# Row factors of two graph attentions: spread over the partitions by TensorE, or put to DRAM once and read back for every partition

## The chip, the cores and the metric

The kernel runs on one core of a Trainium2 chip. The metric is the device time of one launch in microseconds (us), the median of the runs shown. A profile is of one further execution of the same program; its durations are those of that execution.

## The reference

Two layers act on x, 3327 nodes of 256 features, with one graph of 3327 x 3327. Each layer is a graph attention followed by a feed-forward part. Layer 0's attention has two heads of 128 features, layer 1's one head of 256. What matters here is the attention:

```python
# layer 0 (per head); layer 1 is the same with one head, then elu
e = leaky_relu(s1[:, None, :] + s2[None, :, :], 0.2)     # node i, neighbour j
e = where(adj == 1, e, -9e15)
att = softmax(e, axis=1)
h_prime = einsum("ijh,jhc->ihc", att, W3h)
x = x + h_prime
```

Layer 0 goes on with a mixture of 16 experts, two for each token (`silu(h w1) * (h w2)`, then `w3`). Layer 1 goes on with 30 steps of `h + 0.01 tanh(h)`, `h * sigmoid(h)`, layer norm and a 256 x 256 product.

## The kernel before, in words

The 3327 nodes are padded to 26 tiles of 128 (`NT = 26`). `exp(leaky_relu(s1 + s2))` is split so that no exponential is needed for a pair of nodes: for node i and neighbour j the weight is a product of a factor of i, which softmax cancels, with `relu(full_j * row_i - part_j) + part_j`. `row_i = exp(0.8 s1_i)` is the **row factor**. `Scores.finish` computes `row`, `full`, `part` and `minus` with the node on the partition, 128 x 26 x heads.

`attend` does one attention. Its work is cut into **parts**: a group of tiles of nodes i, for one head. Layer 0 has the groups 0-3, 4-9, 10-15, 16-21, 22-25 with two heads each: ten parts, numbered 0 to 9, of 4, 4, 6, 6, 6, 6, 6, 6, 4, 4 tiles. Layer 1 has nine parts, eight of three tiles and one of two. Within a part a loop of 26 **steps** runs over the tiles j of neighbours. A step is one instruction on ScalarE (`e`, L252), one on VectorE (`pT`, L257, which multiplies by the graph's mask `adjT`) and for each tile of the part a product on TensorE (L262), which is two records in the trace:

```python
e  = relu(rb * full_j + minus_j)        # ScalarE, L252; rb: row factors along the free dimension
pT = (e + part_j) * adjT                # VectorE, L257
po[c] += pT[:, c].T @ wh[j]             # TensorE, L262
```

`e` and `pT` have three buffers each, so ScalarE can be three steps ahead of VectorE and VectorE three ahead of TensorE.

In `e` the node i lies along the free dimension, and every one of the 128 partitions needs the same row factors. `row_factors` makes that tile, `rb`: for each tile a product on TensorE of the factor's column, taken 128 times as the stationary operand, with the identity (L221), into a PSUM bank, and for up to four tiles a copy by ScalarE (L225). `rb` has two buffers. The `rb` of part k+1 is made in step 13 of part k. `rb` buffers also take the gathered tokens of the experts (`gathered`, L730): the first of them is asked for while layer 0's attention is still at work.

The results of a part are closed within the steps of the next (`close`, from step 2 on). When both heads of a group are closed in layer 0, `route` follows: a normalization of the group's tiles into the tile `row` (not the row factors; one buffer), whose variance goes to GpSimd for a power (`rstd`, L120) and comes back to VectorE (L127), then a store of `row` to `table_x`, the gate's products on TensorE (L147, L499), a dozen small operations on VectorE that pick two experts, and for each tile two indirect DMAs from GpSimd that write the tokens into the experts' lists (L565). These are held back and let out one by one between the steps.

The graph comes in by groups. `take_graph` lets GpSimd's queue convert a group's rows from int32 to one byte into a DRAM buffer, `in_bytes` (L301), and SyncE's queue reads them back transposed into `adjT` (L311). The buffer is one, so a group's conversion waits for the transposes of the group before. Groups 0 to 2 are asked for before the attention begins; group 3 and 4 after the last list entries of groups 0 and 1.

In layer 1, SyncE's queue stores each finished group of x to `kept`, before x is normalized in place.

A scheduler turns this into one order for each engine. It works from the program's order and its own estimates; an engine then works strictly in that order, waits included. `keep_in_program_order` binds an instruction to its place among the others of its queue.

Of the kernel before, what the change touches and what calls it, by code (L numbers as in the profile page):

```python
# [11 lines left out]
F32 = mybir.dt.float32  # L12
# [8 lines left out]
P = 128  # L21
# [9 lines left out]
def gat_moe_gat_recurrent_ffn(ctx: ExitStack, tc: tile.TileContext, a: dict, out: bass.AP):  # L31
    nc = tc.nc
    N, D = a["x"].shape
    KD = D // P
    NT = (N + P - 1) // P
# [9 lines left out]
    groups0 = [range(0, 4), range(4, 10), range(10, 16), range(16, 22), range(22, 26)]  # L45
    groups1 = [range(max(t - 2, 0), t + 2) for t in range(0, NT, G)]
    groups2 = [range(t, min(t + 3, NT)) for t in range(0, NT, 3)]
# [3 lines left out]
    def rows(t):  # L51
        return P if t < NT - 2 else (REST + 1 - t % 2) // 2
# [44 lines left out]
    ident = const.tile([P, P], F32, name="ident")  # L97
# [85 lines left out]
    class Scores:  # L183
# [9 lines left out]
        def finish(self, t0, t1):  # L193
            nc.scalar.activation(self.full[:, t0:t1], self.s[:, t0:t1, 1], AF.Exp)
            nc.scalar.activation(self.part[:, t0:t1], self.s[:, t0:t1, 1], AF.Exp, scale=ALPHA)
            nc.scalar.activation(self.row[:, t0:t1], self.s[:, t0:t1, 0], AF.Exp, scale=1.0 - ALPHA)
            nc.vector.tensor_scalar(self.minus[:, t0:t1], self.part[:, t0:t1], -1.0, None, op0=ALU.mult)

    quick = []

    def attend(sc, wh, heads, row_groups, per_bank, finish, finished, pools, later, leave=False):

        work, rows_p, ps_r, ps_o = pools
        W = wh.shape[3]  # L210
        most = max(len(ts) for ts in row_groups)
        parts = [(ts, h) for ts in row_groups for h in range(heads)]

        def row_factors(ts, h):

            rb = rows_p.tile([P, most * P], F32, name="rb")
            for c0 in range(0, len(ts), 4):
                some = ts[c0 : c0 + 4]
                p = ps_r.tile([P, 4, P], F32, name="bank")
                for c, t in enumerate(some):  # L220
                    nc.tensor.matmul(  # L221
                        p[:, c, :], lhsT=sc.row[:, t, h : h + 1].to_broadcast([P, P]), rhs=ident,
                        start=True, stop=True,
                    )
                nc.scalar.copy(  # L225
                    rb[:, c0 * P : (c0 + len(some)) * P], p[:, : len(some), :].rearrange("p c q -> p (c q)")
                )
            return rb

        def close(ts, h, po):  # L230

            for c, t in enumerate(ts):
                pr = rows(t)
                r = small.tile([P, 1], F32, name="r")
                nc.vector.reciprocal(r[:pr], po[c][:pr, W - 1 : W])
                finish(t, pr, h, po[c][:pr, : W - 1], r[:pr])
                yield
            if h == heads - 1:
                yield from finished(ts)

        closing = iter(())
        following = row_factors(*parts[0])
        for k, (ts, h) in enumerate(parts):
            n = len(ts)
            rb = following
            acc = [ps_o.tile([P, 512], F32, name=f"acc{q}") for q in range((n + per_bank - 1) // per_bank)]
            po = [acc[c // per_bank][:, (c % per_bank) * W : (c % per_bank + 1) * W] for c in range(n)]
            for j in range(NT):
                if j == NT // 2 and k + 1 < len(parts):
                    following = row_factors(*parts[k + 1])  # L250
                e = work.tile([P, most * P], F32, name="e")
                nc.scalar.activation(  # L252
                    e[:, : n * P], rb[:, : n * P], AF.Relu,
                    scale=sc.full[:, j, h : h + 1], bias=sc.minus[:, j, h : h + 1],
                )
                pT = work.tile([P, most * P], F32, name="pT")
                masked = nc.vector.scalar_tensor_tensor(  # L257
                    pT[:, : n * P], e[:, : n * P], sc.part[:, j, h : h + 1],
                    adjT[:, j // 2, ts[0] * P : (ts[-1] + 1) * P, j % 2], op0=ALU.add, op1=ALU.mult,
                )  # L260
                for c in range(n):
                    nc.tensor.matmul(  # L262
                        po[c], lhsT=pT[:, c * P : (c + 1) * P], rhs=wh[:, j, h, :],
                        start=(j == 0 and c % per_bank == 0), stop=(j == NT - 1),
                        skip_group_check=True,
                    )
                if j >= 2 and (next(closing, later) is later and later and later[0] in quick or later and j % 2 == 0):
                    later.popleft()(masked.ins)
            for _ in closing:
                pass  # L270
            while later and later[0] in quick:
                later.popleft()(None)
            closing = close(ts, h, po)
        if leave:
            return closing
        for _ in closing:
            pass
        while later:
            later.popleft()(None)
# [42 lines left out]
    dram = ctx.enter_context(tc.tile_pool(name="dram", bufs=1, space=bass.MemoryType.DRAM))  # L322
# [35 lines left out]
    with ExitStack() as moe:  # L358
# [16 lines left out]
        H = 2  # L375
        C = D // H
        keep = moe.enter_context(tc.tile_pool(name="keep0", bufs=1))
        wh = keep.tile([P, NT, H, C + 1], F32, name="wh")
        sc = Scores(keep, H)
        ps = moe.enter_context(tc.tile_pool(name="ps0", bufs=4, space=PSUM))  # L380
        ps_o = moe.enter_context(tc.tile_pool(name="ps0o", bufs=2, space=PSUM))
# [99 lines left out]
        run = moe.enter_context(tc.tile_pool(name="edge0", bufs=3))  # L481
        rows_p = moe.enter_context(tc.tile_pool(name="rows0", bufs=2))
# [131 lines left out]
        row = gate.tile([P, MOST, D], F32, name="row")  # L614
# [111 lines left out]
        def gathered(s):  # L726
            if s % 3 == 0 or s == ALWAYS:
                places.append(rows_p.tile([P, MOST * P], F32, name="rb"))
            row = places[-1][:, (s % 3) * D : (s % 3 + 1) * D]
            nc.gpsimd.indirect_dma_start(  # L730
                out=row, out_offset=None, in_=table_x[: EARLY * P, :] if s < FIRST else table_x,
                in_offset=bass.IndirectOffsetOnAxis(ap=which[:, s : s + 1], axis=0),
            )
            return row
# [113 lines left out]
            weights(0)  # L848

        later = deque()  # L850
        closing = attend(sc, wh, H, groups0, 3, add_scaled, route, (run, rows_p, ps, ps_o), later, True)
        ahead.append(gathered(3))
        weights(1)

# [37 lines left out]
    with ExitStack() as st:  # L892
# [3 lines left out]
        wh = s_wh[:, :, :, 2:]  # L896
        sc = Scores(keep, 1, s_wh[:, :, 0, 0:2].rearrange("p t (s h) -> p t s h", h=1))
        nc.vector.memset(wh[:, :, :, D : D + 1], 1.0)
        work = st.enter_context(tc.tile_pool(name="work2", bufs=2))
        ps = st.enter_context(tc.tile_pool(name="ps2", bufs=2, space=PSUM))  # L900
        ps_o = st.enter_context(tc.tile_pool(name="ps2o", bufs=2, space=PSUM))
# [33 lines left out]
        run = st.enter_context(tc.tile_pool(name="edge2", bufs=3))  # L935
        rows_p = st.enter_context(tc.tile_pool(name="rows2", bufs=2))
        fin = st.enter_context(tc.tile_pool(name="fin2", bufs=2))
# [11 lines left out]
        def begin_state(ts):  # L949
# [3 lines left out]
            tiles = [x[:, t, :] for t in ts]  # L953
            normalized(tiles, tiles, S)

        attend(sc, wh, 1, groups2, 1, add_elu, begin_state, (run, rows_p, ps, ps_o), deque())

# [16 lines left out]
    with ExitStack() as st:  # L976
        ps_t = st.enter_context(tc.tile_pool(name="ps3t", bufs=2, space=PSUM))
        ps_o = st.enter_context(tc.tile_pool(name="ps3o", bufs=2, space=PSUM))
# [13 lines left out]
        for step in range(N_STEPS):  # L992
            for ts in groups:
# [28 lines left out]
                if step == N_STEPS - 1:  # L1022
                    here = slice(ts[0] * P, (ts[-1] + 1) * P)
# [55 lines left out]
```

The softmax here doesn't subtract the row's maximum and nothing guards it: scores larger than these inputs give would overflow.

## Time and profile before

| | |
|---|---|
| Median of 3 runs | 2000.29 us (1998.33 to 2000.75) |
| Profiled execution, its own time | 2004.62 us |
| Its span on the core | 2002.9 us |
| Mean granted clock of TensorE | 0.994 |
| Layer 0's attention, on TensorE | about 50 to 395 us |
| Experts | about 395 to 748 us |
| Layer 1's attention | about 793 to 1096 us |
| 30 steps of the last part | from about 1098 us to the end |

The profile counts busy time by engine, cuts the span into 40 slices of about 50 us, and follows the chain of work that ended last back from the end. In a line of a timeline stand the start, the duration, the engine, the line of the kernel (L221), the operation, the names of what is written and read, the count, and in brackets the idle time ahead of it with what ended it. Queue q0 is GpSimd's DMA queue, q1 SyncE's, q10 ScalarE's.

### The profile page before, as it was taken

How to read it: one execution, taken by the hardware profiler on the slowest of the kernel's cores; microseconds unless marked ns; L12 is line 12 of the kernel's file. 1: busy time of each engine (PE TensorE's matmuls, PEld its weight loads, DVE VectorE, ACT ScalarE, POOL GpSimd, SP SyncE). 2: the span in 40 equal slices, each digit the busy share in tenths (PEclk: the TensorE clock that was granted, in tenths of full speed). 3: DMA queues.
4: the chain of work that ended last, by engine and by line, in shares of the span. 5: the costliest groups of instructions: out<-in, count | busy, mean ns of one | idle time of the engine just before them, and what ended most of it. 6: DMA issues, size and time to landing. Idle time of an engine off the chain costs nothing.

```text
span 2002.9 us, 33524 instructions
## 1 busy us (share of the span) xinstructions
PE 1930.9 (96%) x12032; PEld 1750.0 (87%) x12032; DVE 1299.7 (65%) x3827; ACT 1095.5 (55%) x1419; POOL 938.4 (47%) x864
## 2 busy tenths in 40 slices
PE   7999999999999997999999999999999999999998
PEld 6999999989999986888888888888888888888887
DVE  6887888722222226567576777777777777777777
ACT  2967766621111115566555666666666666666664
POOL 3020212443333321001000787787787787787785
PEclk9999999999999998999999999999999999999999
DMA  8978141189999854000001000000000000000003
GB/s 165 119 100 119 10 76 50 39 291 324 351 330 308 297 195 137 9 8 17 9 17 35 1 1 1 1 1 1 1 1 1 1 1 1 1 1 1 1 1 116
DMA packets 139754, 157.08 MB, mean 78 GB/s; under 512 B 52027, under 2 KB 99364, under 8 KB 139586
## 3 DMA queue, kind: packets, MB, share of 16 engines
q1 hardware_dynamic: 123466, 122.05, 19.8%
q0 software_dynamic: 11440, 28.09, 8.1%
q10 hardware_dynamic: 4680, 4.76, 0.7%
q8 instruction: 98, 1.61, 0.3%
q14 instruction: 70, 0.57, 0.1%
HBM read 164.58 MB, written 29.78 MB: 97 GB/s over the span
## 4 chain that ended last, share of the span: by engine, by line
PE 68%; issue 9%; ACT 5%; POOL 5%; DVE 4%; DMA 3%; SPq 0%; another core or an unknown queue 0%; POOLq 0%; DVEq 0%; ACTq 0%
PE po L1014 35%; PE acc L262 23%; PE pt L1008 5%; ACT zT L1010 5%; DVE pT L257 2%; POOL given L831 2%; POOL rb L730 2%; DMA given<-wh,to 2%; PE bank L786 2%; PE acc L827 1%; PE bank L499 1%; PE bank L221 0%; DVE x L913 0%; PE acc L162 0%; POOL rstd L120 0%
## 5 line engine op out<-in xcount | busy, mean ns | idle before, releaser
L1014 PE MATMUL po<-wc,zT 128*128 128x256 f32 x3120 | 705.5, 383 | 21.7 <-ACT zT L1010 21.1
L1014 PEld LDWEIGHTS po<-wc,zT 128*128 128x128 f32 x3120 | 583.1, 190 | 124.1 <-ACT zT L1010 49.7
L252 ACT ACTIVATE e<-rb,minus,full 128x384 f32<-128x384 f32 (+3 forms) x494 | 400.2, 824 | 180.9 <-DVE pT L257 162.7
L1000 POOL TENSOR_TENSOR th<-th,x 128x1024 f32<-128x1024 f32 (+1 forms) x210 | 460.8, 2213 | 64.3 <-ACT th L998 62.7
L257 DVE SCALAR_TENSOR_TENSOR pT<-e,part,adjT 128x384 f32<-128x384 f32 (+3 forms) x494 | 381.1, 776 | 138.1 <-PE acc L262 117.5
L1019 DVE SCALAR_TENSOR_TENSOR x<-po,rr,bb 128x256 f32<-128x256 f32 x780 | 324.9, 478 | 118.3 <-PE po L1014 113.8
L1010 ACT COPY zT<-pt 128x1024 f32<-128x1024 f32 (+1 forms) x210 | 199.0, 947 | 334.0 <-PE pt L1008 334.0
L1006 DVE BATCH_NORM_STATS2 stats<-z 128x6 f32<-128x256 f32 x780 | 283.7, 415 | 117.6 <-ACT z L1001 117.6
L262 PE MATMUL acc<-wh,pT 128*128 128x129 f32 x2704 | 310.4, 276 | 1.8 <-DVE pT L257 1.8
L262 PEld LDWEIGHTS acc<-wh,pT 128*128 128x128 f32 x2704 | 305.2, 192 | 2.5 <-DVE pT L257 2.4
L262 PE MATMUL acc<-s_wh,pT 128*128 128x257 f32 x1352 | 295.3, 380 | 0.8 <-DVE pT L257 0.7
L262 PEld LDWEIGHTS acc<-s_wh,pT 128*128 128x128 f32 x1352 | 255.9, 190 | 37.7 <-DVE pT L257 1.8
L120 POOL TENSOR_TENSOR rstd<-ve,neg_half 128x4 f32<-128x4 f32 (+3 forms) x28 | 30.4, 1086 | 415.7 <-DVE ve L118 332.1
L989 POOL TENSOR_TENSOR rr<-rr,neg_half 128x4 f32<-128x4 f32 (+1 forms) x210 | 208.0, 990 | 17.4
L1001 ACT ACTIVATE z<-th 128x1024 f32<-128x1024 f32 (+1 forms) x210 | 210.6, 1003 | 0.6 <-POOL th L1000 0.5
L998 ACT ACTIVATE th<-x 128x1024 f32<-128x1024 f32 (+1 forms) x210 | 199.3, 995 | 1.9 <-DVE x L127 0.9
L1008 PE MATMUL pt<-ident,z 128*128 128x128 f32 x1560 | 191.6, 274 | 2.5 <-DVE high L944 2.5
L1008 PEld LDWEIGHTS pt<-ident,z 128*128 128x128 f32 x1560 | 179.5, 142 | 14.9 <-issue 2.9
L786 PEld LDWEIGHTS bank<-hT,wh 128*128 128x128 f32 x1280 | 150.7, 194 | 9.2 <-issue 4.8
L786 PE MATMUL bank<-hT,wh 128*128 128x128 f32 x1280 | 151.8, 277 | 6.6 <-issue 2.2
L820 DVE TENSOR_TENSOR pT<-e,bank 128x512 f32<-128x512 f32 x61 | 41.9, 687 | 176.9 <-PE bank L786 124.2
L816 ACT ACTIVATE e<-bank 128x512 f32<-128x512 f32 x61 | 36.4, 597 | 194.1 <-PE bank L786 90.3
(189 smaller groups left out, 1346.4 us busy)
## 6 DMA issues: line engine op xcount, KB each, us to landing
wh<-in_w_dram SPq DMA_DIRECT2D x120, 512.0 KB
first_set<-in_w_dram SPq DMA_DIRECT2D x63, 512.0 KB
in_bytes<-in_adj_dram POOLq DMA_DIRECT2D x3, 2496.0 KB
x<-in_x_dram SPq DMA_DIRECT2D x6, 512.0 KB
kept<-x SPq DMA_DIRECT2D x8, 384.0 KB
old<-kept SPq DMA_DIRECT2D x6, 512.0 KB
out_dram<-x SPq DMA_DIRECT2D x6, 512.0 KB
table_x<-row ACTq DMA_DIRECT2D x3, 768.0 KB
```

Source lines behind the costliest of these rows:

```text
L252: nc.scalar.activation(e[:, : n * P], rb[:, : n * P], AF.Relu, scale=sc.full[:, j, h : h + 1], bias=sc.minus[:, j, h : h + 1],)
L257: masked = nc.vector.scalar_tensor_tensor(pT[:, : n * P], e[:, : n * P], sc.part[:, j, h : h + 1], adjT[:, j // 2, ts[0] * P : (ts[-1] + 1 ...
L262: nc.tensor.matmul(po[c], lhsT=pT[:, c * P : (c + 1) * P], rhs=wh[:, j, h, :], start=(j == 0 and c % per_bank == 0), stop=(j == NT - 1), s ...
L786: nc.tensor.matmul(p[:, f, :], lhsT=w[:, k, f * P : (f + 1) * P], rhs=hT[:, k, :], start=(k == 0), stop=(k == KD - 1),)
L989: nc.gpsimd.tensor_tensor(r[:, :n], r[:, :n], neg_half[:, :n], ALU.pow)
L1000: nc.gpsimd.tensor_tensor(th[:, :n, :], th[:, :n, :], hs, ALU.add)
L1001: nc.scalar.activation(z[:, :n, :], th[:, :n, :], AF.Silu, scale=1.0 / S)
L1006: nc.vector.bn_stats(stats[:, j, :], z[:, j, :])
L1008: nc.tensor.transpose(pt[:, j, k, :], z[:, j, k * P : (k + 1) * P], ident)
L1010: nc.scalar.copy(zT[:, :n, :, :], pt[:, :n, :, :])
L1014: nc.tensor.matmul(po[:, j, :], lhsT=zT[:, j, k, :], rhs=wc[:, k, :], start=(k == 0), stop=(k == KD - 1),)
L1019: nc.vector.scalar_tensor_tensor(x[:, ts[0] + j, :], po[:, j, :], rr[:, j : j + 1], bb, op0=ALU.mult, op1=ALU.add)
```

## The change

`attend` gets a triple, `spread`: the queue for the row factors, the number of parts that still make `rb` as before (`by_dma`), and a place in SBUF for one small tile (`room`). In layer 0 these are GpSimd's queue, 3 and a slice of the router's tile `row`; in layer 1 SyncE's queue, 1 and a tile `low`.

All row factors of a layer are transposed once by TensorE (52 or 26 rows of 128), copied by VectorE to that place and put to DRAM (`factors`). From part `by_dma` on, `rb` is read from there by one DMA, whose source repeats the same rows for all 128 partitions: 128 x 6 x 128 floats for a part of six tiles, 393 KB. The put stands in step 2 of part `by_dma - 1`; the read of the first such part in step 13 of the part before, later ones in step 2 of the part before.

```diff
-    def attend(sc, wh, heads, row_groups, per_bank, finish, finished, pools, later, leave=False):
+    def attend(sc, wh, heads, row_groups, per_bank, finish, finished, pools, later, spread, leave=False):
...
+        queue, by_dma, room = spread
+        factors = dram.tile([NT * heads, P], F32, name=f"factors{heads}")
+
+        def put_factors():
+
+            p = ps_r.tile([P, 512], F32, name="bank")[: NT * heads, :P]
+            nc.tensor.transpose(p, sc.row.rearrange("p t h -> p (t h)"), ident)
+            lines = room()[: NT * heads, :P]
+            nc.vector.tensor_copy(lines, p)
+            tc.keep_in_program_order(queue.dma_start(factors, lines))
 
         def row_factors(ts, h):
 
             rb = rows_p.tile([P, most * P], F32, name="rb")
+            if parts.index((ts, h)) >= by_dma:
+                here = factors[ts[0] * heads + h : ts[0] * heads + h + 1, :]
+                queue.dma_start(
+                    rb[:, : len(ts) * P].rearrange("p (c q) -> p c q", q=P),
+                    bass.AP(tensor=here.tensor, offset=here.offset, ap=[[0, P], [heads * P, len(ts)], [1, P]]),
+                )
+                return rb
...
             for j in range(NT):
-                if j == NT // 2 and k + 1 < len(parts):
+                if j == 2 and k == by_dma - 1:
+                    put_factors()
+                if j == (NT // 2 if k < by_dma else 2) and k + 1 < len(parts):
                     following = row_factors(*parts[k + 1])
...
-        closing = attend(sc, wh, H, groups0, 3, add_scaled, route, (run, rows_p, ps, ps_o), later, True)
+        closing = attend(sc, wh, H, groups0, 3, add_scaled, route, (run, rows_p, ps, ps_o), later, (nc.gpsimd, 3, lambda: row[:, 0, :]), True)
...
-        attend(sc, wh, 1, groups2, 1, add_elu, begin_state, (run, rows_p, ps, ps_o), deque())
+        attend(
+            sc, wh, 1, groups2, 1, add_elu, begin_state, (run, rows_p, ps, ps_o), deque(),
+            (nc.sync, 1, lambda: fin.tile([P, D], F32, name="low")),
+        )
```

## The prediction

> **What bounds the kernel now.** I read the page's busy shares first, then the 40 slices, then the chain that ended last, then stretches of the timeline of TensorE (PE), VectorE (DVE) and GpSimd (POOL) around the row factors.
>
> ```profile
> PE 1930.9 (96%) x12032; PEld 1750.0 (87%) x12032; DVE 1299.7 (65%) x3827; ACT 1095.5 (55%) x1419; POOL 938.4 (47%) x864
> DMA  8978141189999854000001000000000000000003
> ...
> PE po L1014 35%; PE acc L262 23%; PE pt L1008 5%; ACT zT L1010 5%; DVE pT L257 2%; POOL given L831 2%; POOL rb L730 2%; DMA given<-wh,to 2%; PE bank L786 2%; PE acc L827 1%; PE bank L499 1%; PE bank L221 0%; DVE x L913 0%; PE acc L162 0%; POOL rstd L120 0%
> ...
> L221 PE MATMUL bank<-ident,row 128*128 128x128 f32 x156 | 20.2, 276 | 0.0
> L225 ACT COPY rb<-bank 128x512 f32<-128x512 f32 (+2 forms) x25 | 11.6, 485 | 3.8 <-PE bank L221 3.4
> ```
>
> TensorE is the bound nearly everywhere, both attentions (L262) included. L221 spreads the row factors there: 78 tiles, two records each. The DMA digits show that the first four slices (0 to 200 us), where layer 0's attention starts, are full of DMA: that is the graph.
>
> In layer 0's third part TensorE's timeline has its only stop; VectorE's and GpSimd's say why:
>
> ```profile
> 53.32 57.89 PE L262 MATMUL acc<-wh,pT 128*128 128x129 f32 x516 [0.16 <-DVE pT L257]
> 112.29 0.67 PE L147 MATMUL bank<-ident,row 128*128 128x128 f32 x4 [1.08 <-DVE row L127]
> ```
>
> ```profile
> 111.73 1.39 DVE L127 TENSOR_SCALAR row<-x,mv,rstd 128x256 f32<-128x256 f32 x4 [0.93 <-POOL rstd L120]
> ```
>
> ```profile
> 91.19 0.69 POOL L301 DMA_DIRECT2D in_bytes<-in_adj_dram  x1 [41.93 <-DMA adjT<-in_bytes]
> 110.03 1.66 POOL L120 TENSOR_TENSOR rstd<-ve,neg_half 128x4 f32<-128x4 f32 x1 [18.15 <-DVE ve L118]
> ```
>
> VectorE cannot pass L127, which normalizes the first four tiles for the router, until GpSimd's rstd is there; the pT of later steps stand behind it, and TensorE behind them. GpSimd's queue is idle from 92 to 110 us, but its ring is not: the 2.5 MB of graph issued at 91.19 keep queue q0 at 103 to 108% of the DMA engines from 95 to 116 us, and the first transposes that wait for them show at 119.6.
>
> **What the Trainium skill says.** "DMA: Bandwidth & Descriptors", section "Queues, rings and completion order": each DMA engine takes the descriptors of a ring in order. The trace agrees: the gate's weights and bias were issued at 18.84 and 19.56 us, behind a graph piece of 17.93, and q0 moved only packets of 3.3 KB until 35 us; the small ones came at 35 to 37 (44 packets with 0.02 MB from 36 to 37). The same page, "Anatomy of one DMA — SWDGE (gpsimd) path": semaphores are waited for by the issuing sequencer, before dispatch, and a DMA has about 2 us of fixed cost. No row shows that cost alone; the graph's last packets at 119.2 and the transpose at 119.6 to 120 do not contradict it. "TensorE: Matmul & The Clock Gate", Part 1: after an idle window of about 3.4 us the clock is halved, for some 3.4 us of new work. The trace differs on the first figure: stops of 2.21 us (before 401.49) and 2.49 us (before 1098.51) were enough. Afterwards 32 matmuls took 5.47 instead of 3.73 us, and 16 transposes 3.57 instead of 1.91: 1.7 us each time.
>
> **The change part by part.**
>
> *Removed on TensorE, layer 0.* Parts 3 to 9 lose 5x6 + 2x4 = 38 tiles. From L221's start to the next L262 it is 1.34 us for six tiles (159.03 to 160.37) and 0.89 for four, 0.223 each. Those made inside parts 2, 3, 5 (1.34) and 7, 8 (0.89) stand between busy matmuls: 5.8 us. Those inside parts 4 and 6 (2.7 us) coincide with VectorE's routing arithmetic: the chain there runs through pT and the router's small operations and names no L221. Nothing to 2.7 is won; I take 1.3, since the changed order on VectorE puts a pT between more of them.
>
> *Removed on TensorE, layer 1.* Steps are 1.30 us of TensorE against 0.62 of VectorE and 0.71 of ScalarE, so all counts: five times 0.67 and 0.45, 3.8 us. In the changed order the four matmuls of L962 and L970 (eight records, 1.74 us) move from the last part to the front. There they take the place of six tiles (1.34) in a stretch that waits for the first pT anyway (L221 from 793.36, first L262 at 796.28). So another 1.7 are saved at the end. Sum of both layers: 12.6 us.
>
> *Removed on ScalarE:* 20 of L225's 25 copies, 9 us; ScalarE waits for VectorE (162.7 us in L252), so nothing.
>
> *Added on TensorE and VectorE:* two transposes of 0.22 us and two copies of 128 columns (nearest row L479, 0.35). In layer 0 they stand at the very front of part 0: 0.2 us. In layer 1 they fill the wait just named: nothing, 0.2 without it.
>
> *Added on GpSimd's queue, start of layer 0.* The scheduler makes the copy early (VectorE's third step, about 55 us), but the put stands behind both graph pieces in the queue. The changed order on GpSimd reads:
>
> ```
> in_bytes (group 2 of the graph)   waits for transposes; 91.19 in the trace before
> factors<-row (the put)            waits for the copy
> rb<-factors (part 3)              waits for the put's landing
> rstd (L120)                       waits for ve
> lists ...
> ```
>
> The put goes out at 92 and is behind the graph in the ring, which drains at about 118 (table_x, which overlapped its last us before, now comes later). With its completion: 119, from 118.5 to 120.5. Part 3's read waits for that and holds the queue; its issue takes 0.7 to 1.0 (768 rows of graph: 0.69), then rstd 1.0. So VectorE starts L127 at about 121.2, not 111.73; its own wait for the put (row is its source) ends earlier. Nine pT stand before L127 in either order, so nothing covers it: TensorE stops 9.5 us longer (8.5 to 11). It then starts at half clock: 1.7 more. **11.2 us** (9 to 13). Transposes, lists and later graph pieces move along; group 3's transposes end at about 190 and are needed past 255.
>
> *The other reads on GpSimd.* There are two buffers, so each waits until ScalarE has read the factors of the part before the one in work, and lands a few us later, a part (24 to 38 us) ahead of need. Its issue is 0.7 to 1.0 us of a queue that is mostly idle. Parts 5 and 7 have theirs ahead of an rstd, but released about 8 steps (11 us) before it. Parts 6 and 8 delay four lists each by 5 us; nobody waits for a list until 323. Nothing.
>
> *Part 9's read is the exception.* The gathered tokens hold one of the two buffers, so it can only be issued when ScalarE has done part 8. Before, a copy of 0.59 us sat there (367.40). Now: issue 0.9, 262 KB and completion 3.5 (the last gather, 128 KB, was issued until 342.3 and moved until 344), 4.4 together, 3.8 more than the copy. TensorE takes part 9's first pT at about 371.1 (its 208 records counted back from 395.1); with e at 368.02, 0.75 for e and 0.7 for pT it was ready at 369.5, so 1.6 of the 3.8 are covered: 2.2 us (0 to 4), and 1.7 for the clock in case it comes. I take 2.5.
>
> *First expert tile.* Half of its transpose now comes after the last attention matmul: 0.4 us (0 to 0.9).
>
> *SyncE's queue, layer 1.* One put and eight reads among the nine stores of kept. DMA is idle (digits 0), each read is a part (34 us) ahead; a store waits at most for one that is released. Nothing; 0.5 at worst through L127's wait for kept.
>
> **Sum:** -12.6 + 0.2 + 11.2 + 2.5 + 0.4 = **+1.7 us**. The profiled execution took 2004.62 (span 2002.9), so 2006.3; it stands 4.3 above the median of 2000.29, and on the median's scale it is **2002.0**.
>
> **The rivals.**
>
> *Balance (0.52).* As summed, with bounds -12.6-1.4+0.2+9 = -4.8 and -11.3+0.4+13+5.7+0.9+0.5 = +9.2; mostly 1998 to 2006.
>
> *Slower: the read for 128 partitions is itself slow (0.3).* All 128 partitions of a read take the same 2 or 3 KB of DRAM, which no transfer of this size does in the trace. Hidden elsewhere by a part's length, it decides in part 9, once the landing exceeds the copy by more than the 1.6 us of cover. Ten us instead of 4.4 add 5.6 and make the clock drop sure: 2002 + 5.6 + 1.2 = 2009. For it: rows of 512 B. Against: DMA is idle there.
>
> *Faster: the stop at 111 us does not come (0.15),* because the put passes the graph or lands in the middle. Then 11.2 is 0 to 3 and the time 1991 to 1994. Against: the gate's packets, which did not pass.
>
> *The change saves nothing (0.03):* VectorE paces layer 0's steps too, and only layer 1's 5.5 are won: 2009.
>
> **How the numbers follow.** 0.2%, 4 us, is what a measurement of this kernel can tell from no change. Balance gives 0.04 faster, 0.38 same, 0.10 slower; the slow read 0.1 same, 0.2 slower; the faster rival 0.11 and 0.04 same; the last slower. Rounded: faster 0.15, same 0.52, slower 0.33. The range 1996 to 2010 leaves out most of the faster rival and the end of the slow one.
>
> **What would show it.** L127's first wait in the third part grows from 0.93 to about 10 us with POOL rstd or the put as releaser, and L262 after it runs at half clock for some 3 us; q0 shows small packets only at about 118. L221 falls from 156 to 34 records. ScalarE waits about 4 us for a DMA before part 9's first e. Layer 1 is 5 to 6 us shorter. Wrong if L127 starts before 115, or if layer 1 gains under 4.

## The result, and the profile after

The changed kernel takes 2007.41 us (median of 13 runs, 2002.62 to 2014.38); the kernel before, on the same chip, 2001.15 (13 runs, 1997.91 to 2005.59). The ratio is 1.0031, 95% interval [1.0018, 1.0043]: about 6 us slower, more than the 0.2% (4 us) that the prediction takes for the least telling difference, though the interval begins just under it. The forecast was 2002.0 us, with "no change" as the likeliest class. The profiled execution of the changed kernel was the longest of its 13 (2014.38 us, span 2012.4); a second one, profiled later on another chip (x10 below), took 2003.98. Both are used.

On the page (busy shares, chain, groups), these lines answer to those shown of before:

```profile
PE 1930.5 (96%) x11912; PEld 1747.0 (87%) x11912; DVE 1300.6 (65%) x3829; ACT 1088.6 (54%) x1399; POOL 946.4 (47%) x872
...
PE po L1039 35%; PE acc L284 22%; PE pt L1033 5%; ACT zT L1035 5%; PE bank L808 4%; DVE pT L279 2%; PE acc L849 2%; DMA given<-wh,to 2%; DMA wh<-in_w_dram 1%; POOL given L853 1%; POOL rb L752 1%; PE bank L147 1%; PE bank L521 1%; DMA lists<-pair,ati 0%; PE acc L162 0%
```

120 TensorE records are gone, and 20 ScalarE copies, as the change says. TensorE's busy time hardly fell (1930.9 to 1930.5), because work at half clock counts as longer. (Half clock: the profile gives the share of TensorE's full clock that was granted, and in these stretches it is 0.50.) The line that spread the factors, now L241, is left with 34 records (groups by line):

```profile
L241 PE MATMUL bank<-ident,row 128*128 128x128 f32 x34 | 4.1, 275 | 0.0
L222 PE MATMUL bank<-ident,row 128*52 128x128 f32 (+1 forms) x2 | 0.6, 278 | 0.3 <-ACT row L196 0.3
```

The rest is in layer 0's third part. GpSimd's timeline (start, duration, operation; in brackets the idle time before it and what ended it):

```profile
90.21 0.69 POOL L323 DMA_DIRECT2D in_bytes<-in_adj_dram  x1 [42.17 <-DMA adjT<-in_bytes]
90.89 0.56 POOL L225 DMA_DIRECT2D factors<-row  x1
118.22 0.87 POOL L232 DMA_DIRECT2D rb<-factors  x1 [26.77 <-issue]
119.10 1.05 POOL L120 TENSOR_TENSOR rstd<-ve,neg_half 128x4 f32<-128x4 f32 x1
```

The put (L225) is issued right behind 2.5 MB of graph in the same ring (the row of transfers that one queue has issued and not yet done); the read that needs it (L232) stands at the head of GpSimd's queue until 118.22; the rstd behind it runs at 119.10, where it ran at 110.03 before. The page's table of transfers gives the put 26.7 us to its landing, which is at about 117.6. VectorE and then TensorE take it on:

```profile
120.19 1.38 DVE L127 TENSOR_SCALAR row<-x,mv,rstd 128x256 f32<-128x256 f32 x4 [9.81 <-POOL rstd L120]
```

```profile
120.66 1.12 PE L147 MATMUL bank<-ident,row 128*128 128x128 f32 x4 [9.87 <-DVE row L127]
121.57 1.50 PE L284 MATMUL acc<-wh,pT 128*128 128x129 f32 x6
122.86 1.73 PE L521 MATMUL bank<-gate_w,hT 128*128 128x16 f32 x8
...
129.63 8.51 PE L284 MATMUL acc<-wh,pT 128*128 128x129 f32 x74
```

TensorE stops 9.87 us instead of 1.08. The second loss is in the durations. Before, the same work showed:

```profile
113.64 1.06 PE L499 MATMUL bank<-gate_w,hT 128*128 128x16 f32 x8
...
117.44 8.51 PE L262 MATMUL acc<-wh,pT 128*128 128x129 f32 x74
```

From L147 to the start of the run of 74 matmuls it is 8.97 us (120.66 to 129.63) where it was 5.15 (112.29 to 117.44), and the eight of L521 (L499 before) show 1.73 us where they had 1.06. That is half clock, and it costs 3.8 us.

L127 depended on the put in a second way: it overwrites `row`, from which the put is read. Had only the rstd been free of the read, L127 would still have waited for the put, until about 117.6 instead of 120.19: an estimate from the landing above.

Part 9 has the other new wait. ScalarE's timeline, first before, where it does not wait, then after; then the issue on GpSimd's and what TensorE felt of it:

```profile
367.40 0.59 ACT L225 COPY rb<-bank 128x512 f32<-128x512 f32 x1
368.02 3.79 ACT L252 ACTIVATE e<-rb,minus,full 128x512 f32<-128x512 f32 x5
```

```profile
380.87 4.50 ACT L274 ACTIVATE e<-rb,minus,full 128x512 f32<-128x512 f32 x6 [4.39 <-DMA rb<-factors]
```

```profile
376.68 0.84 POOL L232 DMA_DIRECT2D rb<-factors  x1 [17.43 <-ACT d L579]
```

```profile
382.52 1.16 PE L284 MATMUL acc<-wh,pT 128*128 128x129 f32 x8 [1.80 <-DVE pT L279]
```

Counted from the first to the last start of an attention matmul, layer 0's attention takes 341.7 us before, 353.4 in the first profile of after and 348.7 in the second one; layer 1's takes 299.4, 295.5 and 295.6.

What sets the two profiles of the same kernel apart is again the clock. In both it is half for 13.7 us about the stop of part 2. In the first it is half three times more in layer 0's attention, 3.4 us each, and in the second and in the profile of before it is not. The windows view of the first (window and length; busy time and count of PE, PEld, DVE, ACT and POOL; clock; DMA share and GB/s):

```profile
115.60:129.30 13.70, 8.64 (x42) 8.61 (x42) 3.88 (x7) 3.01 (x4) 1.92 (x2) 0.50 0.95 161
204.30:207.70 3.40, 3.40 (x18) 3.40 (x19) 1.47 (x2) 0.59 (x1) 0.00 (x0) 0.50 0.68 231
282.80:286.20 3.40, 3.40 (x18) 3.40 (x18) 1.18 (x2) 0.59 (x1) 0.00 (x0) 0.51 0.68 231
368.20:371.60 3.40, 3.15 (x14) 3.15 (x15) 2.93 (x8) 2.61 (x4) 0.00 (x0) 0.50 0.00 0
```

The last of these begins ahead of part 9's read. TensorE's 78 matmuls there, in the first profile and in the second:

```profile
368.45 10.47 PE L284 MATMUL acc<-wh,pT 128*128 128x129 f32 x78 [0.69 <-DVE pT L279]
```

```profile
365.10 8.98 PE L284 MATMUL acc<-wh,pT 128*128 128x129 f32 x78 [0.69 <-DVE pT L279]
```

So 1.5 us of what part 9 seems to lose in the first profile is not the read's. The wait of 0.69 us is new itself: it stands in all seven profiles in which TensorE no longer makes part 9's factors (the two of after, x2, x3, x7, x8 and x11), and half clock followed it in two of them, this one and x11's.

### The profile page after: what moved, and what is told of

Read it like the earlier page. It is cut to its first block, busy times and chain, and to the rows that moved or that the text cites. A ratio compares the mean times of both kernels' runs of the same rounds, so it can differ in the third digit from the quotient of the medians.

```text
span 2012.4 us, 33304 instructions
## 1 busy us (share of the span) xinstructions
PE 1930.5 (96%) x11912; PEld 1747.0 (87%) x11912; DVE 1300.6 (65%) x3829; ACT 1088.6 (54%) x1399; POOL 946.4 (47%) x872
## 4 chain that ended last, share of the span: by engine, by line
PE 70%; issue 8%; ACT 5%; DMA 4%; DVE 4%; POOL 3%; SPq 0%; POOLq 0%; DVEq 0%; ACTq 0%
PE po L1039 35%; PE acc L284 22%; PE pt L1033 5%; ACT zT L1035 5%; PE bank L808 4%; DVE pT L279 2%; PE acc L849 2%; DMA given<-wh,to 2%; DMA wh<-in_w_dram 1%; POOL given L853 1%; POOL rb L752 1%; PE bank L147 1%; PE bank L521 1%; DMA lists<-pair,ati 0%; PE acc L162 0%
## 5 line engine op out<-in xcount | busy, mean ns | idle before, releaser
L284 PE MATMUL acc<-wh,pT 128*128 128x129 f32 x2704 | 315.8, 279 | 4.1 <-DVE pT L279 4.1
L284 PEld LDWEIGHTS acc<-wh,pT 128*128 128x128 f32 x2704 | 310.8, 195 | 5.2 <-DVE pT L279 5.2
L284 PE MATMUL acc<-s_wh,pT 128*128 128x257 f32 x1352 | 294.5, 380 | 1.3 <-DVE pT L279 1.2
L284 PEld LDWEIGHTS acc<-s_wh,pT 128*128 128x128 f32 x1352 | 256.3, 190 | 39.4 <-DVE pT L279 3.3
```

The source lines that it names most:

```text
L284: nc.tensor.matmul(po[c], lhsT=pT[:, c * P : (c + 1) * P], rhs=wh[:, j, h, :], start=(j == 0 and c % per_bank == 0), stop=(j == NT - 1), s ...
```

## The experiments

Theory A: the loss is in two places, part 2's stop (the put behind the graph in one ring, a read that waits for it, an rstd behind the read) and part 9's late read; taking the transposes away does gain. Rival B: reading the factors for 128 partitions costs time wherever it happens. A ratio is to the kernel before on the same chip, and microseconds beside it are the ratio's distance from 1 times 2000 us. x1 to x4 shared one chip, x7 to x10 a second, x11 to x13 a third; a comparison across these groups goes through two ratios.

**x10: the changed kernel again.**

> The changed kernel itself, for the comparison with the others on one chip. All theories: 1.001 to 1.005 of before; the stop at part 2 near 10 us, the wait ahead of part 9's first e near 4.4 us.

Ratio 1.0039 [1.0025, 1.0052], stop 10.41 us. Its five runs had a mean granted clock of 0.9898, the nine of before beside it 0.9941. The 13.7 us of half clock at part 2's stop are 0.0034 of the 2002 us span, most of that difference: the loss is in part a loss of clock, though 5 to 6 of the 13.7 us lie within the stop and cost nothing.

**x1: the change in layer 1 alone.** `(nc.gpsimd, 3, ...)` becomes `(nc.gpsimd, 99, ...)` in layer 0's call: no part is read by DMA there.

> Layer 0 makes every part's factors on TensorE as before; only layer 1 keeps the put and the reads on SyncE's queue. Theory A (layer 1 gains, layer 0 loses by one stop at part 2 and one late read at part 9): 3.5 to 5.5 us shorter than before, so about 10 us shorter than the changed kernel; VectorE's L127 in part 2 begins again near 112. Theory B (a read of the factors for 128 partitions costs time wherever it runs): layer 1 has five reads to layer 0's six, so about as much is lost here as in layer 0, and this is equal to or longer than before.

0.9987 [0.9977, 0.9996]: 2.6 us shorter, a little under A's range. L127 is back at 111.50. B, which would have it equal or longer, fails, by its time only narrowly: the reads in layer 1 cost nothing that outweighs the gain. Layer 1's attention took 295.5 us, as in the changed kernel, where it was 299.4.

**x2: the change in layer 0 alone.** `(nc.sync, 1, ...)` becomes `(nc.sync, 99, ...)`.

> Layer 1 makes every part's factors on TensorE as before; layer 0 keeps the put and the reads on GpSimd's queue. Theory A: the 11.3 us that attention 0 lost in the profiled execution stay, less what is noise, so 8 to 12 us longer than before, and 3 to 5 longer than the changed kernel. Theory B: each layer loses its share, so this is 1 to 4 us longer than before.

1.0068 [1.0055, 1.0081]: 13.6 us longer, above A's range, far above B's. In its profile the graph's piece was issued at 94.17 instead of 90.21, so the put landed later and the stop was 12.49 us. Part 9 was slower too (x11 below shows how). This profile is of the longest of its five runs (2027.31 us; the median is 2019.86).

**x3: ScalarE issues layer 0's transfers.**

```diff
-... later, (nc.gpsimd, 3, lambda: row[:, 0, :]), True)
+... later, (nc.scalar, 3, lambda: row[:, 0, :]), True)
```

> The changed kernel with layer 0's put and reads issued by ScalarE instead of GpSimd. Theory A: GpSimd's rstd of part 2 is no longer held behind the read, and the put no longer lies behind the 1.7 MB of the graph in GpSimd's ring, so L127 begins near 111 and the stop is that of before; what is left is part 9's late read (3 to 5 us) and a wait of up to 3 us of ScalarE for the put's landing. 6 to 10 us shorter than the changed kernel, 0 to 4 shorter than before. Theory B: the queue doesn't matter, within 2 us of the changed kernel.

1.0037 [1.0025, 1.0049]: no shorter than the changed kernel. A missed the time here, and B named it; the traces show that B's reason is not the cause. The put landed in 7 us and L127 began at 111.53, without the stop. Another stop of the same size took its place, in ScalarE's queue:

```profile
96.75 0.31 ACTq L225 DMA_DIRECT2D factors<-row  x1
103.98 0.40 ACTq L232 DMA_DIRECT2D rb<-factors  x1
...
112.80 0.58 ACT L148 COPY hT<-bank 128x512 f32<-128x512 f32 x1 [1.13 <-PE bank L147]
125.39 0.38 ACTq L514 DMA_DIRECT2D table_x<-row  x1
125.81 0.58 ACT L148 COPY hT<-bank 128x512 f32<-128x512 f32 x1 [12.43 <-DMA adjT<-in_bytes]
```

The write of table_x, issued at 113.15 in the kernel before, now waits until 125.39, for a transpose of the graph by the profile, and ScalarE's second hT copy stands behind it. TensorE stops for that copy, and works at half clock after it:

```profile
126.45 1.89 PE L521 MATMUL bank<-gate_w,hT 128*128 128x16 f32 x8 [9.85 <-ACT hT L148]
128.18 10.32 PE L284 MATMUL acc<-wh,pT 128*128 128x129 f32 x74
```

The trace names the counter on which each transfer of the SyncE and ScalarE queues reports its landing: there are eight, taken in turn in the program's order. In the kernel before the write of table_x takes the sixth, last used by a transpose issued at 84.41. With the put and the read on ScalarE it takes the eighth, last used by the transpose issued at 120.84, whose last report is at 125.31, just ahead of the write. That this shift is the cause is argued from these numbers; no run changes the counter alone.

**x4: part 9's factors by TensorE again, all else as changed.**

```diff
-            if parts.index((ts, h)) >= by_dma:
+            if by_dma <= parts.index((ts, h)) < len(parts) - (heads == 2):
...
-                if j == (NT // 2 if k < by_dma else 2) and k + 1 < len(parts):
+                if j == (NT // 2 if k < by_dma or heads == 2 and k + 2 == len(parts) else 2) and k + 1 < len(parts):
```

> The changed kernel, but the factors of layer 0's last part are made on TensorE, in the middle of part 8, as before. Theory A: the 4.4 us that ScalarE waits for the read ahead of that part's first e go, and 4 transposes of 0.22 us come back: 3 to 4 us shorter than the changed kernel; the stop at part 2 stays. Theory B: one read of six away, so about 1 to 2 us shorter.

1.0026 [1.0015, 1.0036], against 1.0031 of the changed kernel: A's 3 to 4 us are not seen, and the difference is inconclusive by itself. The wait ahead of part 9 is gone (part 8's rstd to the router's last: 49.92 us, 52.47 in the changed kernel), but this profile's stop in part 2 was longer, 12.40 us, with 19.3 instead of 13.7 us for what follows up to the next router matmul (L565, L543 before): 5.7 us lost to half clock.

**x8 and x9: the put ahead of the graph's next piece** (x9 also with part 9 as in x4).

```diff
...
-            for ts in groups0[1:3]:
-                behind = take_graph(ts, behind)
+            behind = take_graph(groups0[1], behind)
+            pf = ps.tile([P, 512], F32, name="bank")[: NT * H, :P]
+            nc.tensor.transpose(pf, sc.row.rearrange("p t h -> p (t h)"), ident)
+            lines0 = hold.tile([P, P], F32, name="lines0")[: NT * H, :]
+            nc.vector.tensor_copy(lines0, pf)
+            with tc.issue_after(behind):
+                put0 = nc.gpsimd.dma_start(factors0, lines0)
+            behind = put0.ins
+            behind = take_graph(groups0[2], behind)
```

> The changed kernel, but layer 0's factors are turned when the projection is done and put by GpSimd's queue ahead of the graph part that the changed kernel puts them behind (issued near 47 instead of 91 us); the reads are as in the changed kernel. Theory A (what holds GpSimd is the put's landing behind the graph in the same ring): the read of part 3 no longer waits for a landing, L127 begins near 112 instead of 120, the stop and its half clock are those of before; part 9's read stays late. 8 to 13 us shorter than the changed kernel, 2 to 6 shorter than before. Theory B (the reads themselves, wherever they stand, hold GpSimd or the transfers): within 3 us of the changed kernel.

> As the kernel with the early put, and the factors of layer 0's last part are made on TensorE as before. Theory A: both losses are gone and the gains stay: 3 to 4 us shorter than with the early put alone, 6 to 10 us shorter than before. Theory B: 1 to 2 us shorter than the changed kernel.

1.0101 [1.0084, 1.0118] and 1.011 [1.0094, 1.0126]: 20 to 22 us longer, the opposite of what A said, and x9 is not shorter than x8. Part 2's stop is gone in both (TensorE's L147 waits 1.08 and 1.09), but the whole attention starts 24 us late. TensorE's and ScalarE's timelines of x8:

```profile
77.55 60.77 PE L286 MATMUL acc<-wh,pT 128*128 128x129 f32 x516 [24.11 <-DVE pT L281]
```

```profile
74.93 1.07 ACT L247 COPY rb<-bank 128x512 f32<-128x512 f32 x2 [25.01 <-DMA in_bytes<-in_adj_dram]
```

The edit was at fault: hold is a pool that is given back before the attention, so the first rb copy, which takes that memory, waits for everything that still reads it, the put included. The profile names the graph's piece of 47.64 as the releaser; the put, issued at 50.89, lies right behind it in the ring and took 23.7 us to land, until about 74.6; and x11, where only its memory is changed, shows that it was the put. It is the same mechanism one piece earlier.

**x11 and x12: the same, with the lines in a tile that stays** (`keep.tile` for `hold.tile`; x12 has part 9 as in x4).

> The early put again, but its lines are staged in a tile that stays allocated through attention 0, so that the first rb copy has no memory to wait for (in the kernel with the early put it waited 25 us for the put's landing). Theory A: the first part begins near 53, L127 near 111 with no stop, part 9's read costs 1 to 2.5 us: 4 to 8 us shorter than before. Theory B (reads themselves cost): no shorter than before.

> As the one before it in this list (lines staged in a tile that stays), and layer 0's last part made on TensorE as before. Theory A: 1 to 2.5 us shorter than that one, and within 3 us of the kernel that makes no factors: 6 to 9 us shorter than before. Theory B: no shorter than before.

x11: 0.9989 [0.998, 0.9998]; x12: 0.9959 [0.9943, 0.9975]. With the put out of the way the change gains, x11 less than A said (2.2 us), x12 as it said (8.2). The intervals do not overlap: reading part 9's factors late instead of making them, the only difference, costs about 6 us here, more than A said. In x11's profile the time from part 8's rstd to the router's last is 56.5 us, in x12's 50.2. As in the first profile of after, 1.6 of these 6.3 us are half clock in the 78 matmuls ahead of the read (10.62 us). Then TensorE's timeline in x11:

```profile
369.39 1.16 PE L286 MATMUL acc<-wh,pT 128*128 128x129 f32 x8 [1.73 <-DVE pT L281]
...
380.19 2.05 PE L286 MATMUL acc<-wh,pT 128*128 128x129 f32 x16 [0.17 <-DVE pT L281]
383.18 1.16 PE L286 MATMUL acc<-wh,pT 128*128 128x129 f32 x8 [0.94 <-DVE pT L281]
384.67 1.16 PE L286 MATMUL acc<-wh,pT 128*128 128x129 f32 x8 [0.33 <-DVE pT L281]
386.16 2.05 PE L286 MATMUL acc<-wh,pT 128*128 128x129 f32 x16 [0.34 <-DVE pT L281]
```

The late read itself costs TensorE 1.73 us. But ScalarE and VectorE then have no lead, and each step of eight matmuls (1.16 us) waits for its pT: a step comes every 1.49 us until 389.9. In x10 the engines caught up at once (160 matmuls without a wait from 383.75) and part 9 cost 1.1 us (51.05 us for the same stretch, 49.96 before). What decides between the two was not found; the profile of x2 falls into the same step, x8's does not.

**x7: nothing made, put or read.**

```diff
-                if j == 2 and k == by_dma - 1:
-                    put_factors()
...
-                    following = row_factors(*parts[k + 1])
+                    following = row_factors(*parts[k + 1]) if k + 1 < by_dma else rb
```

> No factors are put, read or made after the parts that TensorE makes (part 2 in layer 0, the first part in layer 1); later parts use the last ones made, so this leaves out that computation. Theory A: the bound on what taking the transposes away can bring, without any transfer: 9 to 13 us shorter than before, and within 3 us of the kernel with the early put and part 9 on TensorE. Theory C (VectorE or ScalarE paces the attention in the stretches where TensorE no longer makes factors, and TensorE waits instead): under 7 us shorter than before.

0.9956 [0.9942, 0.997]: 8.8 us shorter, the bound on what the removal can give, a little under A's range. Layer 0's attention takes 334.2 us (7.4 less than before), layer 1's 295.6 (3.8 less). C, which had TensorE wait for the others instead and so under 7 us, does not fit the two attentions, though the interval reaches to 6.

**x13: ScalarE issues the put alone** (reads on GpSimd's queue, part 9 as in x4).

```diff
-            tc.keep_in_program_order(queue.dma_start(factors, lines))
+            tc.keep_in_program_order((nc.scalar if heads == 2 else queue).dma_start(factors, lines))
```

> The put stays at its place in part 2 but is issued by ScalarE; the reads stay on GpSimd's queue; layer 0's last part is made on TensorE as before. Theory A: with ScalarE as the put's issuer it landed within 7.2 us (issue 96.75, landed by 103.98), so GpSimd's read no longer holds the rstd of part 2, and the stop of 10 us goes: 5 to 9 us shorter than before. Theory D (what stopped the kernel with all of layer 0's transfers on ScalarE is the shift of the completion counters by the added DMAs, which makes the table_x write wait for a transpose): a stop of about 10 us between the two hT copies of part 2 stays even with one added DMA, and it is 2 to 8 us longer than before.

0.9946 [0.993, 0.9962]: 10.8 us shorter than before, more than A said, and 0.8% under x4, from which it differs in the put's queue alone. GpSimd's timeline, then TensorE's:

```profile
104.38 0.87 POOL L232 DMA_DIRECT2D rb<-factors  x1 [11.44 <-DMA factors<-row]
109.36 1.66 POOL L120 TENSOR_TENSOR rstd<-ve,neg_half 128x4 f32<-128x4 f32 x1 [4.11 <-DVE ve L118]
```

```profile
111.53 0.76 PE L147 MATMUL bank<-ident,row 128*128 128x128 f32 x4 [1.00 <-DVE row L127]
```

The put, issued at 96.69 while the graph filled the DMA engines, had landed by 104.38, so the read is out of the way 4 us before the rstd. D as it was worded falls: with one added transfer the write of table_x is issued at 112.48, without a wait. It now takes the seventh counter, last used by a transpose issued at 87.01, so the argument made for x3 stands. This is the shortest version of all, and its interval overlaps x7's: as far as these intervals tell, it has all that the removal can bring.

## Why the prediction was right and wrong

The time lay inside the range, and the mechanisms were the ones named, but the sum was 4 to 5 us short and the likeliest class was wrong. The nearest single number, 2009 of the rival "slow read", came near by chance: its mechanism did not occur. By its steps:

- *Removed on TensorE, layer 0* (predicted 7.1 us): 7.4 by x7. Right.
- *Removed on TensorE, layer 1* (5.5): 3.5, under the 4 that the prediction set as its own limit. Two terms failed. The busy time that left the attention was 4.7 us (from 299.34 in 796.2 to 1096 before to 294.66 in x10), not 5.5, and waits for pT rose by 0.5. And the front was not free: L987 and L995 moved into it as said, but first L241 to first L284 is 3.36 us (806.41 to 809.77), where before it was 2.92. The reads are not to blame: x7, without any, gains 3.8 within the attention.
- *The put behind the graph and the stop* (9.5): TensorE stopped 8.8 us longer, and each link was where it was put: read at 118.22 (predicted 119), L127 at 120.19 (121.2), rstd as its releaser. x13 shows it: against x4 only the put's queue is changed, and the stop is 1.00 us instead of 12.40.
- *Half clock after the stop* (1.7): 3.8 in the profiled execution, 5.7 after x4's longer stop. This is the term that was mis-sized. The 1.7 was read off after stops of 2.2 and 2.5 us and carried over to one four times as long, with other work behind it. How much of the difference is the stop's length and how much the work is open: after x3's stop of 9.85 us, with long runs of matmuls behind it, 2.7 us were lost (1.89 and 10.32 us where before shows 0.96 and 8.51).
- *Part 9's read*: the wait of ScalarE was predicted at 4.4 us and is 4.39. Its price (2.5) seems to hold in the first profile (52.47 us from part 8's rstd to the router's last, 49.92 without the read), but by luck: 1.5 us are the half clock ahead of the read, which leaves 1.1 for the read itself, as in x10. Between x11 and x12 it was 6 us: the bound of 4 for the plain delay left out that three engines in a chain may not win their lead back, and the bound for the clock looked only behind the wait.
- *Other reads, SyncE's queue, added transposes*: nothing, as said. The rival of a slow read falls with x1 and x13: part 9's landed in 4.1 us in the changed kernel.

In x10's profile the stop is 9.3 us longer than before and the work behind it 3.3 (121.07 to 129.51), so the terms are -7.4 - 3.5 + 9.3 + 3.3 + 1.1: +2.8 us. That execution, the shortest of its five, took 2003.98 us, 2.95 above the median of before beside it. In the first profile the two are 8.8 and 3.8, and the three further stretches of half clock come to about 1.7 us each, an estimate from 3.4 us of full work at half speed. The median, +6, lies between the two; how executions that were not profiled divide it is not known.

The rival "the stop does not come", 1991 to 1994 us, is what x13 turned the change into: 0.9946 of 2000.29 is 1989.5 us, with part 9 made on TensorE.

## What to carry to other kernels

A small transfer whose landing something waits for must not stand behind a large one in the same ring: price it at the time the ring needs to drain, and ask what the engine that waits holds up. Issue it from another engine's queue and look again, at that engine's own waits. When a long stop is added, do not take the price of its half clock from a short one (1.7 us after stops of 2.2 and 2.5 us here, 2.7 to 5.7 after stops of 9.85 to 12.40), and take the work that follows as slow until the trace shows it fast. Where a late buffer hits a chain of engines, the chain may lose its lead for several steps. And before one profile is taken for the price of a change, compare the granted clock in its stretches with that of a second profile.

## What was not expected of the hardware

- The half clock lasted longer than the Trainium skill says. "TensorE: Matmul & The Clock Gate", Part 1, has the full clock back after about 3.4 us of sustained work. After part 2's stop in the changed kernel the clock was half until 129.3, 8.6 us after TensorE's work began again, and after x4's stop of 12.40 us it reaches into the run of 74 matmuls (9.96 instead of 8.51 us). TensorE was hardly idle in either; it ran mixed short work. In x3, after a stop of 9.85 us and with long runs of matmuls behind it, the clock was half until 131.9, 5.5 us after the work began again.
- A short wait can be followed by half clock in one execution and not in the next. The 78 matmuls above had the same wait of 0.69 us ahead of them in both profiles of the changed kernel and took 10.47 and 8.98 us; 32 matmuls at the experts' start took 5.47 us after a stop of 2.21 us in the profile of before and 3.84 after one of 2.20 us in x12's. So stops of 2.2 us, which the prediction found to be enough, were enough in that profile and not always. In the traces the half clock lasts 3.4 us or about a whole multiple of it (10.2, 13.7 and 20.5 us after the long stops of x3, the changed kernel and x4).
- The same 26 KB took 26.7 us to land behind the graph in GpSimd's ring, and at most 7.7 from ScalarE's (96.69 to 104.38 in x13) while that graph was still moving. "DMA: Bandwidth & Descriptors", section "Queues, rings and completion order", says that each DMA engine takes turns between the queues that have work for it, a packet at a time; the two figures agree with that.
